# The first batch's last two slots as seven-product slots, and down_w's rounding behind them

## The chip, the cores and the metric

The kernel runs on one core of a Trainium2 chip. The metric is the device time of one execution in microseconds (us), lower is better; the time given for the kernel before is the median of three runs. One further execution was recorded by the hardware profiler, and all rows of the profile come from it.

The core has five engines with queues of their own: TensorE (PE: matmuls; its weight loads, PEld, overlap them), VectorE (DVE), ScalarE (ACT), GpSimd (POOL) and SyncE (SP, which here issues nearly all DMAs). Each runs its instructions in the order in which the kernel wrote them; semaphores order the engines against each other.

## The reference

```python
x (4,1024,512) f32, cond (4,128), norm_w (512,128), up_w (4096,512), down_w (512,2048)
scale = cond @ norm_w.T + 1.0
ms = mean(x * x, axis=-1)
h = x * (scale[:, None, :] * rsqrt(ms + 1e-6))
u = h @ up_w.T                       # 4096 columns: val, gate
val, gate = split(u, 2, axis=-1)
h = val * gelu(gate)                 # exact gelu, 2048 columns
s = 127 / max(|h|, axis=-1);  hq = clip(round(h * s), -128, 127) / s
m = mean(|down_w|);  wq = clip(round(down_w / m), -1, 1) * m
y = hq @ wq.T + x
```

So there is an up projection in full precision, a gated activation, and a down projection of whole numbers between -128 and 127 by weights of -1, 0 and 1.

## The kernel before, in words

**Tiles and loops.** The four batches of 1024 tokens are worked on one after the other, each in two halves of 512 tokens (`TOK`). The 2048 hidden columns are cut into 16 *slots* (`NJ`), slot j being 128 value rows and the 128 gate rows that belong to them. An fp32 product is made from f16 parts: each operand is split into a high and a low part, and high x low, low x high and high x high are added up, over a contraction of 512 in four pieces of 128. That is 12 matmuls (128x128 weights, 512 tokens) for one product of a slot: gate or value, first or second half, 48 matmuls a slot. This plain form is `plain` (matmuls L601), called by `plain_half` (product `pg` of the gate, Gelu on ScalarE L629, product `pv` of the value, then VectorE's value x gate, L633).

**The seven-product form.** From batch 1 on a slot is `slot`: the four products are seen as a 2x2 block product (two blocks of the contraction, two halves of tokens by value and gate) and formed from seven products of half the contraction, of 6 matmuls each (`product`, L586), 42 matmuls a slot. They need seven combinations of the weights and seven of the tokens. Three of each are the blocks themselves, four are sums or differences. The products 2 and 3 of a slot are done in the slot behind it. PSUM banks go by tag: A has two, B one, E two; the plain form uses the same ones (`pg` of the first half in B, of the second in A, `pv` in E; slot 6 has one of its own).

**Batch 0 is plain, and prepares the rest.** While its slots run, the other engines make what the later batches need. `first_batch(j)` is the order written out by hand for slot j; each of its steps works a few slots ahead:
- `w_range(j+3)`: the largest |weight| of each up_w row (VectorE reduce, L290), a power of two near it, and its inverse (L155, L297, L303); `w_gain` L317. `w_scale` (ScalarE, L329) scales the rows by it.
- `w_rows`: high part (ScalarE, L353) and low part (VectorE, L354) of the scaled rows, into a row tile (`ROW_SLOT`, a slot of the big buffer H), and a DMA transpose on SP (L355) into the slot's weight tile.
- `s_sums` (GpSimd, L380 to L383), `s_high` (ScalarE, L392), `s_low` (GpSimd, L396): the four weight sums with their high and low parts, and `s_spill` (SP, L400), which writes the whole set to `s_dram`; from there `s_load_x` and `s_load_y` fetch it for each later slot, two slots ahead.
- batch 1's tokens (`Tokens`, four pieces, at slots 6, 8, 10, 12 and the one after each): load, norm (Square on ScalarE, L520), scale, sums, high and low parts, and a transpose into batch 1's token tile.
- down_w: its eight pieces are loaded early, |down_w| is summed (`d_sum`, ScalarE, L448, two passes for two pieces), the mean is formed at slot 4 (`d_mean`, matmul L457), and in slots 5 to 12 each piece is rounded (`d_round`, ScalarE, L464) and put as sign into fp8 (`d_put`, ScalarE, L473), with a transpose into `wd`, the tile of the down projection's weights (L475).
- `pair_max`: the running largest |h| of the batch's tokens, by pairs of slots (`LARGEST`, VectorE, L719 to L726).

**The later batches.** In each slot of a later batch the spare time of VectorE and ScalarE is filled with the quantisation of the batch before, the running largest and the next tokens; `Filler` holds these steps in order and gives each place x, y, z of a slot as many as a budget in us admits. The down projection of the batch before comes in slots 10 to 13 of the batch.

Of the kernel before, what the change touches and what calls it, by code (L numbers as in the profile page):

```python
# [9 lines left out]
F32 = mybir.dt.float32  # L10
# [41 lines left out]
def glu_quant_kernel(  # L52
# [30 lines left out]
    DVE.memset(neghalf, -0.5)  # L83
    emask = cpool.tile([P, 2], I32, name="emask")
    DVE.memset(emask, EXPONENT)
    undo_up = cpool.tile([P, 2], F32, name="undo_up")
    DVE.memset(undo_up, 1.0 / W_UP)
    unmagic = cpool.tile([P, 1], F32, name="unmagic")
    DVE.memset(unmagic, -MAGIC)
    one = cpool.tile([P, 1], F32, name="one")  # L90
# [45 lines left out]
        "p (c w f) -> p c w f", c=7, w=2  # L136
    )
    A21 = R[:, 0, 6144 : 6144 + 768].bitcast(F16).rearrange("p (n w f) -> p n w f", n=3, w=2)

    def s_tile(g):  # L140


        if g >= NJ:
            return SXY[:, (g + 1) % 2]
        return S_more if g % 3 == 2 else SXY[:, g % 3]
# [129 lines left out]
    def wn(j):  # L275
        return H[:, W_EARLY.get(j, W_SLOT[j % 3])]
# [3 lines left out]
    def w_load(j, ts=(1, 0)):  # L280
# [3 lines left out]
        for t in ts:  # L284
            SP.dma_start(out=wn(j)[:, t], in_=up_v[j][:, t])

    def w_largest(j, t0=0, t1=2):
        t = slice(t0, t1)
        am = sm.tile([P, 2], F32, name=f"wam_{j}_{t0}", tag="wam")[:, t]
        DVE.tensor_reduce(am, wn(j)[:, t], AX.X, ALU.max, apply_absolute_value=True)  # L290
        return am

    def w_factor_steps(j, am, t0=0, t1=2):
        t = slice(t0, t1)
        pow2_floor(am)
        yield
        DVE.scalar_tensor_tensor(  # L297
            sw[:, j, t], am, 2.0**-100, undo_up[:, t], ALU.max, ALU.mult
        )
# [3 lines left out]
        DVE.reciprocal(iv[j][:, t], sw[:, j, t])  # L303
# [41 lines left out]

    def w_rows(j):

        v = H[:, ROW_SLOT.get(j, 15 + j % 2)].bitcast(F16).rearrange("p t d -> p (t d)")  # L350
        n = v.rearrange("p (n w f) -> p n w f", n=4, w=2)
        f = wn(j).rearrange("p t (n f) -> p (t n) f", n=2)
        ACT.copy(n[:, :, 0], f)  # L353
        DVE.tensor_tensor(n[:, :, 1], f, n[:, :, 0], ALU.subtract)  # L354
        SP.dma_start_transpose(  # L355
            s_tile(j)[:, 3:7].rearrange("p n w (k f) -> p (n w k) f", k=2), v
        )

    def w_high(j, ts=(1, 0)):
# [17 lines left out]
    def s_sums(j):  # L377
        v = wn(j).rearrange("p t (n f) -> p t n f", n=2)
        a11, a12, a21, a22 = v[:, 1, 0], v[:, 1, 1], v[:, 0, 0], v[:, 0, 1]
        POOL.tensor_tensor(sf[:, 0], a21, a22, ALU.add)  # L380
        POOL.tensor_tensor(sf[:, 2], a11, a21, ALU.subtract)
        POOL.tensor_tensor(sf[:, 1], sf[:, 0], a11, ALU.subtract)
        POOL.tensor_tensor(sf[:, 3], a12, sf[:, 1], ALU.subtract)  # L383
# [14 lines left out]
    def s_spill(j):  # L398
        def out(c0, c1, v):
            SP.dma_start(  # L400
                out=s_dram[j, :, c0 * 2 * HALF : c1 * 2 * HALF],
                in_=v.rearrange("p c w f -> p (c w f)"),
            )

        s = s_tile(j)
        if j < ROWS:
            out(0, C_ALL, s)
            return
        out(0, 3, s[:, 0:3])
        out(4, C_ALL, s[:, 4:])  # L410
        out(3, 4, A21[:, j % 3 : j % 3 + 1])

    def s_load(g, c0, c1, turn=False):
        s, d = s_tile(g)[:, c0:c1], s_dram[g % NJ, :, c0 * 2 * HALF : c1 * 2 * HALF]
# [2 lines left out]
        else:  # L417
            SP.dma_start(out=s.rearrange("p c w f -> p (c w f)"), in_=d)

    def s_load_x(g):  # L420
        s_load(g, Y_TO, C_ALL)
        s_load(g, 0, Y_FROM, True)

    def s_load_y(g):
# [10 lines left out]
    def d_part(n):  # L435
        return R[:, 1, n * HF : (n + 1) * HF]
# [18 lines left out]
    def d_mean(part):  # L455
# [2 lines left out]
        DVE.tensor_scalar(wmean, pm, 1.0 / (D * FF), 1e-5, ALU.mult, ALU.max)  # L458
        DVE.reciprocal(wsc, wmean)

    def d_round(n):

        dn = d_part(n)
        ACT.activation(dn, dn, AF.Copy, scale=wsc, bias=MAGIC)  # L464

    tn = []

    def d_put(n):
        _, u, y = d_at(n)
        if y == 0:  # L470
            tn.append(wpool.tile([P, HF], BF16, name=f"tn_{n}", tag="v"))
        t8 = tn[-1].bitcast(F8).rearrange("p (f y) -> p f y", y=2)
        ACT.activation(t8[:, :, y], d_part(n), AF.Sign, bias=unmagic, saturate=False)  # L473
        if y:
            SP.dma_start_transpose(wd[:, n // 4, u], tn[-1])  # L475

    def w_block(name):
        k, y = W_AT[name]
# [98 lines left out]

    TERMS = [(w, 1 - w, k) for w in (1, 0) for k in range(2)] + [(0, 0, k) for k in range(2)]

    def product(c, g, ps, start, stop):  # L580
        s = s_tile(g)[:, PLACE[c]]
        s = s.rearrange("p w (k f) -> p w k f", k=2)
        tv = t_view(g // NJ)
        o = ps.rearrange("p (a t) -> p a t", t=P)
        for n, (w, l, k) in enumerate(TERMS):
            PE.matmul(  # L586
                o, s[:, w, k, :], tv[:, :, c, l, k, :],
                start=start and n == 0, stop=stop and n == len(TERMS) - 1,
                skip_group_check=True,
            )  # L590

    def plain(j, t, h, ps):

        gate, a21, a22 = a_parts(j)
        a = [gate[:, 0], gate[:, 1]] if t else [a21, a22]
        a = [v.rearrange("p w (k f) -> p w k f", k=2) for v in a]
        terms = [(w, 1 - w, k) for k in range(NK) for w in (1, 0)]
        high = [(0, 0, k) for k in range(NK)]
        terms = high + terms if j < 2 else terms + high
        for n, (w, l, k) in enumerate(terms):  # L600
            PE.matmul(  # L601
                ps, a[k // 2][:, w, k % 2, :], XP[:, l, k, h * TOK : (h + 1) * TOK],
                start=n == 0, stop=n == len(terms) - 1,
            )

    sg = {0: sg0}

# [449 lines left out]
    def second_part():  # L1057
# [18 lines left out]
    LARGEST = {  # L1076
        4: ((0, 0), (0, 1)), 5: ((1, 0), (1, 1)), 8: ((2, 0), (2, 1)), 10: ((3, 0), (3, 1)),
        12: ((4, 0), (4, 1)), 14: ((5, 0), (5, 1)), 15: ((6, 0), (6, 1)),
    }
    toks = {}  # L1080

    def next_tokens(j):

# [9 lines left out]
    def first_batch(j, sc):  # L1093

        if j + 2 <= LATE:
            w_load(j + 4)
        if j >= 4:
            next_tokens(j + 2)
        t = toks.get(j)
        odd = t is not None and j not in TOKENS  # L1100
        n = j + 2
        rows = LATE <= n < NJ
        if j + 1 < LATE:
            s_sums(j + 1)
        elif rows:
            s_sums(n)
# [6 lines left out]
        for i, h in LARGEST.get(j, ()):  # L1113
            for f in pair_max(0, i, h):
                f()
        if n < LATE:
            w_scale(n)
            w_rows(n)
        if j + 1 < LATE:
            s_all(j + 1)  # L1120
        if t and not odd:
            t.norm()
        for m in D_ROUND.get(j, ()):
            d_round(m)
            d_put(m)
        if t and not odd:
            t.scale(sc)
            t.sums()
# [5 lines left out]
        if odd:  # L1134
            t.turn()
        plain_half(j, 1)
        if j == 3:
# [5 lines left out]
        own = rows and j + 1 >= LATE  # L1143

        def next_rows():
            if LATE <= j + 3 < NJ:
# [5 lines left out]
        if own:  # L1152
            s_high(n)
            s_low(n, POOL)
        if not odd:
            next_rows()
        if own:
# [4 lines left out]
            w_load(j + 5)  # L1162
        for n in D_SUM.get(j, ()):
            d_sum(n)
        if j in (NJ - 3, NJ - 1):
            s_load_x(NJ + (j - NJ + 3) // 2)
            s_load_y(NJ + (j - NJ + 3) // 2)


    def second_slot():  # L1170
# [62 lines left out]
    for n in D_SUM[2]:  # L1233
        d_sum(n)

    for j in range(3, NJ):
        if j == 5:
            sc = cond_load_scale(1)
        if j == 6:
            cond_bring(1, sc)  # L1240
        first_batch(j, sc if j >= 5 else None)

# [90 lines left out]
    state = {}  # L1333
    for b in range(1, B):
        dve, act = Filler(), Filler()
        gains(b)
        am = am_tile(b - 1)
        dq = state[b - 1] = sm.tile([P, 2 * NA], F32, name=f"dq_{b}", tag="dq")
        last_pair = NJ // 2 - 1
        for h in range(2):  # L1340
            add_pair(
# [38 lines left out]
        for j in range(NJ):  # L1380
# [11 lines left out]
            act_left = {"x": 2.7, "y": 2.2 if down else 1.1, "z": 0}  # L1392

            def run(p):
                nonlocal left
# [34 lines left out]

            def loads():
                if NJ + 2 <= g + 2 < B * NJ:
                    s_load_x(g + 2)
                if NJ + 2 <= g + 1 < B * NJ:
                    s_load_y(g + 1)


# [187 lines left out]
```

## Time and profile before

| what | value |
|---|---|
| median of 3 runs (lowest, highest) | 725.66 us (725.57, 725.80) |
| span of the profiled execution | 724.0 us |
| busy: PE, DVE, ACT, POOL | 716.5, 584.2, 397.6, 201.6 us |
| TensorE's share of the chain that ended last | 98% |
| a slot in plain form, on that chain | 4 x 2.59 = 10.36 us |
| slots 14 and 15 of batch 0 | 163.44 to 184.16 us |

The profile gives no total of its own beside the span, which runs from the first to the last recorded instruction; the runs' times hold what lies around it as well, 1.66 us by the median.

Rows of a timeline read: start, length, engine, line, operation, written tile <- read tiles, shape and type, and in brackets the idle time before it with what ended it. "x12" is a run of 12 such instructions in one row. Lines of tiles drop the buffer's number: H is the big buffer of activations and weights rows, SXY and R hold the slots' weight tiles. A row of the chain of waits reads: start, length, what. TensorE's granted clock is 1.00 in the stretches that are shown.

### The profile page before, as it was taken

To read this page: it belongs to the slowest core of one execution; us is meant where nothing else is said; L and a number is where in the kernel's file an instruction comes from. 1 tells how busy PE (TensorE), PEld (TensorE's weight loads), DVE (VectorE), ACT (ScalarE), POOL (GpSimd) and SP (SyncE) were. 2 spreads that over 40 slices of the span, in tenths; PEclk is the share of its full clock that TensorE was granted. 3 is DMA by queue.
4 is the path that set the end of the run, shared out by engine and by line. 5 is a ranking of instruction groups with operands and counts; after the bars stand their busy time and mean duration, and the time that the engine had idled before them with its cause. 6 is when DMAs were issued, how large, how long until landed. Compare 5 with 4: busy or idle time off the path is not lost.

```text
span 724.0 us, 10200 instructions
## 1 busy us (share of the span) xinstructions
PE 716.5 (99%) x3678; PEld 359.9 (50%) x3678; DVE 584.2 (81%) x824; ACT 397.6 (55%) x625; POOL 201.6 (28%) x207
## 2 busy tenths in 40 slices
PE   7999999999999999999999999999999999999998
PEld 3544444444444446655444445666444444445854
DVE  8977999984698899887689897687678888755896
ACT  6768868861337674554335676544433665333473
POOL 1579788882100034440000030360020000000120
PEclk9999999999999999999999999999999999999999
DMA  9579999996654564977846646766955455453253
GB/s 317 190 231 271 300 287 251 276 229 152 117 103 102 132 150 127 208 174 167 174 102 103 131 102 176 200 155 159 216 105 103 101 104 100 102 101 97 103 174 119
DMA packets 224191, 117.85 MB, mean 163 GB/s; under 512 B 186486, under 2 KB 196871, under 8 KB 224140
## 3 DMA queue, kind: packets, MB, share of 16 engines
q1 hardware_dynamic: 223850, 116.87, 66.1%
q8 instruction: 29, 0.48, 0.3%
q10 hardware_dynamic: 290, 0.33, 0.1%
q14 instruction: 22, 0.18, 0.1%
HBM read 49.50 MB, written 23.09 MB: 100 GB/s over the span
## 4 chain that ended last, share of the span: by engine, by line
PE 98%; DMA 1%; ACT 0%; SPq 0%; issue 0%; DVE 0%; ACTq 0%
PE A L586 34%; PE E L586 17%; PE pg L601 11%; PE pv L601 11%; PE po L880 9%; PE B L586 9%; PE po_end L832 4%; DMA H<-in_x_dram 1%; PE ptx L981 1%; PE pv L648 0%; PE po_B L880 0%; PE pg L648 0%; PE pw L339 0%; PE po_A L880 0%; PE po_E L880 0%; ACT R L947 0%
## 5 line engine op out<-in xcount | busy, mean ns | idle before, releaser
L586 PEld LDWEIGHTS <-SXY 128*128 128x128 f16 x2016 | 196.9, 98 | 231.3 <-issue 0.6
L586 PE MATMUL A<-R,SXY 128*128 128x512 f16 x1152 | 266.0, 379 | 0.0
L586 PE MATMUL E<-R,SXY 128*128 128x512 f16 x576 | 140.0, 379 | 0.1
L688 DVE SCALAR_TENSOR_TENSOR H<-A,sg,t 128x512 f32<-128x512 f32 x48 | 36.0, 750 | 67.9 <-PE A L586 67.7
L740 POOL PARTITION_ALL_REDUCE am<-R x8 | 14.3, 1793 | 234.0 <-DVE R L726 234.0
L804 DVE TENSOR_TENSOR H<-H,am 128x1024 f32<-128x1024 f32 x64 | 76.1, 1215 | 0.0
L601 PEld LDWEIGHTS <-SXY 128*128 128x128 f16 x486 | 47.4, 98 | 57.4 <-DVE SXY L372 0.5
L701 ACT ACTIVATE t<-t,sg 128x512 f32<-128x512 f32 x48 | 34.6, 721 | 67.8 <-DVE t L698 67.7
L586 PE MATMUL B<-R,SXY 128*128 128x512 f16 x288 | 70.0, 379 | 0.0
L724 DVE TENSOR_REDUCE gm<-H 128x512 f32<-128x1024 f32 x56 | 69.0, 1233 | 1.0
L601 PE MATMUL pg<-R,SXY 128*128 128x512 f16 x252 | 58.0, 379 | 0.0
L601 PE MATMUL pv<-R,SXY 128*128 128x512 f16 x234 | 54.4, 380 | 0.0
L685 ACT ACTIVATE t<-B,sg 128x512 f32<-128x512 f32 x48 | 33.0, 687 | 36.3 <-PE B L586 36.3
L880 PE MATMUL po<-wd,R 128*128 128x256 fp8e4 x416 | 52.5, 273 | 0.0
L490 POOL TENSOR_SCALAR ssq<-ssq 128x2 f32<-128x2 f32 x12 | 4.3, 354 | 171.2 <-ACT xt L520 122.1
L668 ACT COPY t<-A 128x512 f32<-128x512 f32 x48 | 27.9, 582 | 39.8 <-PE A L586 39.5
L880 PEld LDWEIGHTS <-R 128*128 128x128 bf16 (+1 forms) x448 | 43.8, 98 | 9.0
L680 ACT COPY v<-E 128x512 f32<-128x512 f32 x48 | 28.1, 585 | 30.9 <-PE E L586 27.7
L675 ACT COPY B<-A 128x512 f32<-128x512 f32 x48 | 27.4, 572 | 30.5 <-PE A L586 30.0
L707 DVE SCALAR_TENSOR_TENSOR H<-v,sg,t 128x512 f32<-128x512 f32 x48 | 38.5, 802 | 6.6 <-ACT t L701 6.6
L812 ACT ACTIVATE H<-H 128x1024 f32<-128x1024 f32 x38 | 39.9, 1050 | 7.1 <-DVE H L804 7.1
L726 DVE TENSOR_TENSOR R<-R,gm 128x512 f32<-128x512 f32 x56 | 42.2, 753 | 1.3
(205 smaller groups left out, 986.8 us busy)
## 6 DMA issues: line engine op xcount, KB each, us to landing
SXY<-s_dram SPq DMA_DIRECT2D x48, 256.0 KB, 3.0
s_dram<-SXY SPq DMA_DIRECT2D x18, 384.0 KB, 3.3
H<-in_L_cond_up_w_dram SPq DMA_DIRECT2D x13, 512.0 KB, 5.7
SXY<-s_dram SPq DMA_DIRECT2D x48, 128.0 KB, 3.2
xr<-in_x_dram SPq DMA_DIRECT2D x19, 256.0 KB, 3.0
out_dram<-xr SPq DMA_DIRECT2D x19, 256.0 KB, 2.6
H<-in_x_dram SPq DMA_DIRECT2D x8, 512.0 KB, 6.7
R<-in_L_cond_down_w_dram SPq DMA_DIRECT2D x8, 512.0 KB, 7.4
```

Of the source, the lines that this page charges most:

```text
L586: PE.matmul(o, s[:, w, k, :], tv[:, :, c, l, k, :], start=start and n == 0, stop=stop and n == len(TERMS) - 1, skip_group_check=True,)
L601: PE.matmul(ps, a[k // 2][:, w, k % 2, :], XP[:, l, k, h * TOK : (h + 1) * TOK], start=n == 0, stop=n == len(terms) - 1,)
L685: ACT.activation(cur["t1"], pb, AF.Gelu, scale=gain(g, 1))
L688: DVE.scalar_tensor_tensor(h_half(g - 1, 0), prev["A"], gain(g - 1, 0), prev["t1"], ALU.mult, ALU.mult)
L701: ACT.activation(prev["t2"], prev["t2"], AF.Gelu, scale=gain(g - 1, 1))
L707: DVE.scalar_tensor_tensor(h_half(g - 1, 1), prev["v"], gain(g - 1, 0), prev["t2"], ALU.mult, ALU.mult)
L724: DVE.tensor_reduce(gm[0], v, AX.X, ALU.max, apply_absolute_value=True)
L726: return [largest, lambda: DVE.tensor_tensor(m, m, gm[0], ALU.max)]
L804: DVE.tensor_tensor(v, v, r.to_broadcast([P, 2, TOK]), ALU.mult)
L812: ACT.activation(v, v, AF.Copy, bias=MAGIC)
L832: PE.matmul(po.rearrange("p (y c o) -> p y c o", c=2, o=P), q[:, a, h, j], wd8[:, :, j // n, j % n, :, y0:y1].rearrange("p c o y -> p y c o"),
L880: PE.matmul(po, w[:, j], m, start=start and j == 0, stop=stop and j == n - 1, skip_group_check=True,)
```

## The change

Slots 14 and 15 of batch 0 (`FAST = NJ - 2`) go through `slot` instead of `plain_half`. What moves for it:
- Token sums of batch 0: four combinations, high and low, in `T0`, which is the memory of `wd`; they are formed at slots 4 to 14 (`T0_STEPS` and `first_fast`) by VectorE, GpSimd and ScalarE. The three plain combinations are read where they stand (`XP`).
- Weight sums of slots 14 and 15 are formed on VectorE instead of GpSimd, and turned by DMA transposes from SBUF (`s_turn`), beside the spill. `w_rows` of these two turns three of its four parts.
- `wd` is thus not free before slot 15. down_w is fetched again, piece by piece, and rounded and signed from slot 14 to slot 19 (`first_fast`, and `D_LATE` in ScalarE's Filler), with the transposes at slots 16, 17, 18 and 20, between the loads (`D_MOVES`).
- From weights 3 on (`BY_SUM`) the range is taken from the sum of |w| of a row instead of its largest: two Abs with accumulation on ScalarE in place of VectorE's reduce. Their elementwise output goes to the row tile of `row_place(j)`. The gain of two slots is formed in one instruction.
- Batch 1's tokens come one slot earlier (5, 7, 9, 11), some of the running largest a slot earlier or later.

```diff
+    FAST = NJ - 2
+    T0 = wd.bitcast(F16).rearrange("p a b c d -> p (a b c d)")
...
+    BY_SUM = 3
+
+    def row_place(j):
+        return H[:, ROW_SLOT.get(j, 15 + j % 2)]
+
     def w_largest(j, t0=0, t1=2):
         t = slice(t0, t1)
         am = sm.tile([P, 2], F32, name=f"wam_{j}_{t0}", tag="wam")[:, t]
+        if j >= BY_SUM:
+            for n in range(2):
+                jk = row_place(j).bitcast(F16)[:, n, :D]
+                ACT.activation(jk, wn(j)[:, n], AF.Abs, accum_out=am[:, n : n + 1])
+            return am
         DVE.tensor_reduce(am, wn(j)[:, t], AX.X, ALU.max, apply_absolute_value=True)
         return am
...
     def w_gain(j):
-        DVE.tensor_tensor(sg0[:, j, :], sw[:, j, :], dx[:, 0:1].to_broadcast([P, 2]), ALU.mult)
+        if j < 3:
+            DVE.tensor_tensor(sg0[:, j, :], sw[:, j, :], dx[:, 0:1].to_broadcast([P, 2]), ALU.mult)
+        elif j % 2 == 0 or j == NJ - 1:
+            c = slice(j - 1, j + 1)
+            DVE.tensor_scalar(sg0[:, c], sw[:, c], dx[:, 0:1], None, ALU.mult)
...
+    def s_turn(j):
+        for n in range(2):
+            SP.dma_start_transpose(
+                s_tile(j)[:, 2 * n : 2 * n + 2].rearrange("p c w (k f) -> p (c w k) f", k=2),
+                s_rows[j][n].rearrange("p c w f -> p (c w f)"),
+            )
...
+    FIRST = {0: (0, 0), 1: (2, 0), 2: (2, 1)}
+
+    def operand(b, c, l, k):
+        if b:
+            return t_view(b)[:, :, c, l, k, :]
+        if c in FIRST:
+            k0, h = FIRST[c]
+            v = XP[:, l, k0 + k, h * TOK : (h + 1) * TOK]
+        else:
+            v = T0[:, c - 3, l, k]
+        return v.rearrange("p (a t) -> p a t", t=P)
...
-    D_ROUND = {5: (0, 1), 6: (2,), 7: (3,), 9: (4,), 10: (5,), 11: (6,), 12: (7,)}
+    D_LATE = [
+        ((0, "x"), d_round, 2), ((0, "x"), d_sign, 2), ((0, "y"), d_round, 3),
+        ((1, "x"), d_sign, 3), ((1, "x"), d_round, 4), ((1, "y"), d_sign, 4),
+        ((2, "x"), d_round, 5), ((2, "x"), d_sign, 5), ((2, "y"), d_round, 6),
+        ((3, "x"), d_sign, 6), ((3, "x"), d_round, 7), ((3, "y"), d_sign, 7),
+    ]
+    D_MOVES = {
+        0: ((d_turn, 0),),
+        1: ((d_turn, 1), (d_fetch, 6)),
+        2: ((d_turn, 2), (d_fetch, 7)),
+        4: ((d_turn, 3),),
+    }
+    T0_STEPS = {
+        (4, 0): [lambda: t0_whole(0, 0, 0), lambda: t0_whole(1, 0, 1)],
+        (4, 1): [lambda: t0_sum(2, 1, 0, ALU.subtract)],
+        (5, 0): [lambda: t0_high(2, 1)],
+        (6, 0): [lambda: t0_low(2, 1)],
+        (6, 1): [lambda: t0_whole(2, 2, 1, POOL)],
+        (8, 0): [lambda: t0_sum(1, 2, 1, ALU.subtract)],
+        (8, 1): [lambda: t0_high(1, 3)],
+        (9, 1): [lambda: t0_low(1, 3)],
+        (10, 0): [lambda: t0_sum(0, 1, 0, ALU.add)],
+        (10, 1): [lambda: t0_high(0, 2)],
+        (11, 0): [lambda: t0_low(0, 2)],
+        (12, 1): [lambda: t0_whole(3, 2, 0, POOL)],
+        (13, 0): [lambda: t0_sum(3, 3, 0, ALU.subtract)],
+    }
     D_MEAN = 4
-    TOKENS = {6: 0, 8: 1, 10: 2, 12: 3}
+    TOKENS = {5: 0, 7: 1, 9: 2, 11: 3}
...
+    def first_fast(j):
+
+        last = j == NJ - 1
+
+        def x():
+            if last:
+                d_round(1)
+                d_sign(0)
+            else:
+                d_round(0)
+
+        def y():
+            if last:
+                d_sign(1)
+            else:
+                t0_high(3, 0)
+
+        def z():
+            if not last:
+                t0_low(3, 0)
+            largest(j)
+
+        slot(j, x, y, z)
+        if last:
+            s_load_x(j + 2)
+            d_fetch(4)
+            d_fetch(5)
+        else:
+            d_fetch(2)
+            d_fetch(3)
...
-    for j in range(3, NJ):
+    for j in range(3, FAST):
...
+    for j in range(FAST, NJ):
+        first_fast(j)
```

`t0_whole` and `t0_sum` are one add or subtract of 128x1024 f32 each, `t0_high` a copy to f16 on ScalarE, `t0_low` the difference between the sum and its high part on VectorE. `D_MOVES` steps run inside `s_load_x` between its two loads; `d_sign` writes what `d_put` wrote, and `d_turn` is its transpose.

More of the change, by code (lines that the diff above doesn't have):

```diff
@@ L459, in d_mean, with d_fetch, d_sign, d_turn @@
         DVE.reciprocal(wsc, wmean)
[L461 to L475 removed]
+    dn = {}
+    tn = {}
+    def d_fetch(n):
+        if n == 2:
+            v = H[:, NJ].rearrange("p h t -> p (h t)")
+        else:
+            tag = ("xn", "xt", None, "nx", "xn", "xt", "nx", "xn")[n]
+            v = wpool.tile([P, HF], F32, name=f"dn_{n}", tag=tag, bufs=1)
+        c, u, _ = d_at(n)
+        SP.dma_start(out=v, in_=down_w[c * P : (c + 1) * P, u * HF : (u + 1) * HF])
+        dn[n] = v
+    def d_round(n):
+        ACT.activation(dn[n], dn[n], AF.Copy, scale=wsc, bias=MAGIC)
+    def d_sign(n):
+        y = n % 2
+        if y == 0:
+            tn[n // 2] = wpool.tile([P, HF], BF16, name=f"tn_{n}", tag="xr")
+        t8 = tn[n // 2].bitcast(F8).rearrange("p (f y) -> p f y", y=2)
+        ACT.activation(t8[:, :, y], dn[n], AF.Sign, bias=unmagic, saturate=False)
+    def d_turn(m):
+        SP.dma_start_transpose(wd[:, m // 2, m % 2], tn[m])
     def w_block(name):
@@ L604, in plain, with t0_whole, t0_sum, t0_high @@
             )
+    TMP = [R[:, 1, n : n + 2 * TOK].rearrange("p (k t) -> p k t", k=2) for n in (7168, 5376, 3584)]
+    TMP.append(H[:, 15])
+    def t0_whole(m, k0, h, eng=DVE):
+        v = XP[:, :, k0 : k0 + 2, h * TOK : (h + 1) * TOK]
+        eng.tensor_tensor(TMP[m], v[:, 0], v[:, 1], ALU.add)
+    def t0_sum(o, m, l, op, eng=DVE):
+        eng.tensor_tensor(TMP[o], TMP[m], TMP[l], op)
+    def t0_high(o, c):
+        ACT.copy(T0[:, c, 0], TMP[o])
+    def t0_low(o, c, eng=DVE):
+        eng.tensor_tensor(T0[:, c, 1], TMP[o], T0[:, c, 0], ALU.subtract)
     sg = {0: sg0}
@@ L1105, in first_batch @@
         elif rows:
-            s_sums(n)
+            s_sums(n, DVE if n >= FAST else POOL)
         if j + 3 < NJ:
@@ L1120, in first_batch @@
             s_all(j + 1)
+        if j + 2 == FAST:
+            s_high(FAST)
+            s_low(FAST, POOL)
+            s_turn(FAST)
+        if j == 12:
+            d_fetch(0)
         if t and not odd:
             t.norm()
-        for m in D_ROUND.get(j, ()):
-            d_round(m)
-            d_put(m)
         if t and not odd:
             t.scale(sc)
-            t.sums()
+            if j < 11:
+                t.sums()
         if j + 2 > LATE and j + 5 < NJ:
@@ L1133, in first_batch @@
             t.low(DVE)
-        if odd:
+        if odd and j + 2 < FAST:
             t.turn()
         plain_half(j, 1)
+        for f in T0_STEPS.get((j, 1), ()):
+            f()
+        if j + 2 == FAST:
+            s_spill(FAST)
+        if j + 2 > FAST:
+            s_high(j + 2)
+            s_low(j + 2, POOL)
+            s_turn(j + 2)
+            d_fetch(1)
+            s_spill(j + 2)
+            toks[j - 1].turn()
         if j == 3:
@@ L1142, in first_batch @@
             d_mean(part)
-        own = rows and j + 1 >= LATE
+        own = rows and j + 1 >= LATE and not ahead
+        rows = rows and not ahead
         def next_rows():
@@ L1335, in glu_quant_kernel @@
         dve, act = Filler(), Filler()
-        gains(b)
+        if b > 1:
+            gains(b)
         am = am_tile(b - 1)
         dq = state[b - 1] = sm.tile([P, 2 * NA], F32, name=f"dq_{b}", tag="dq")
+        if b == 1:
+            for at, f, n in D_LATE:
+                act.add(at, 1.1, lambda now, f=f, n=n: f(n))
         last_pair = NJ // 2 - 1
```

90 lines of the change are left out of this document (60 added, 30 removed).

## The prediction

> **What bounds the kernel now.** I read the page's head and chain first, then the chain of waits around the two slots, then the same chain and the engines' timelines where the preparation of the first batch is densest. The page (engine rows: busy time, share of the span, instructions):
>
> ```profile
> span 724.0 us, 10200 instructions
> ...
> PE 716.5 (99%) x3678; PEld 359.9 (50%) x3678; DVE 584.2 (81%) x824; ACT 397.6 (55%) x625; POOL 201.6 (28%) x207
> ...
> PE 98%; DMA 1%; ACT 0%; SPq 0%; issue 0%; DVE 0%; ACTq 0%
> ```
>
> TensorE carries 98% of the chain that ends last: a matmul taken away is time won, and any new wait of TensorE is time lost. The chain at the two slots that change (start, length, what; us):
>
> ```profile
> 163.44 2.59 PE pg L601 x12
> 166.03 2.59 PE pv L601 x12
> ...
> 181.57 2.59 PE pv L601 x12
> 184.16 1.29 PE A L586 x6
> ```
>
> Slots 14 and 15 run from 163.44 to 184.16 without a gap, eight products of 12 matmuls, 2.59 us each.
>
> **The saving.** The two slots go from 2 x 48 matmuls (four products of 12) to 2 x 42 (seven of 6), and the operands keep their shape, so one matmul keeps its price: 2.59 / 12 = 0.216 us plain, 1.29 / 6 = 0.215 us in the scheme. 12 x 0.216 = 2.59 us. If TensorE waits nowhere, 725.66 - 2.59 = 723.07 us. The profiled execution spans 724.0, so 1.66 us lie around the span of the median run; I take them as unchanged.
>
> What it costs must therefore be a wait of TensorE. The engines' busy time by stretch (window, then PE, PEld, DVE, ACT, POOL, granted clock, DMA share, GB/s):
>
> ```profile
> 60.00:70.00 10.00, 10.00 (x49) 4.67 (x48) 7.63 (x13) 9.90 (x18) 8.61 (x9) 1.00 0.99 304
> 70.00:80.00 10.00, 10.00 (x50) 4.57 (x49) 9.86 (x14) 8.69 (x12) 9.15 (x12) 1.00 1.09 290
> 170.00:180.00 10.00, 10.00 (x48) 4.56 (x47) 4.94 (x7) 1.37 (x2) 0.38 (x1) 1.00 0.50 108
> ```
>
> At 60 to 70 us ScalarE has 0.1 us of 10 to spare, at 170 to 180 it has 8.6. The change adds ScalarE work in the first place and moves other ScalarE work to the second.
>
> **Weight ranges on ScalarE.** From slot 3's weights on, one reduce of VectorE becomes two Abs with accumulation on ScalarE. The nearest rows are the Square pair of the token norms, the same 128x512 with accumulation, and the reduce it replaces:
>
> ```profile
> 83.77 0.62 ACT L520 ACTIVATE xt<-xn 128x512 f32<-128x512 f32 x1
> ...
> 85.00 1.14 ACT L464 ACTIVATE R<-R,wsc 128x1024 f32<-128x1024 f32 x1
> ```
>
> ```profile
> 47.60 1.21 DVE L290 TENSOR_REDUCE wam<-H 128x2 f32<-128x1024 f32 x1
> ...
> 52.90 1.20 DVE L354 TENSOR_TENSOR H<-H 128x1024 f16<-128x1024 f32 x1
> ```
>
> The Square pair at 83.77 occupies 1.23 us until the next one at 85.00; I take 1.23 for each range. 13 x 1.23 = 16.0 us go onto ScalarE, 13 x 1.21 = 15.7 us leave VectorE. Through slots 5 to 12 this is nearly paid by the 16 rounding passes that leave ScalarE there (1.14 each, the row at 85.00). In slots 2 to 4 nothing leaves. So I follow ScalarE's queue there:
>
> ```profile
> 42.77 1.33 ACT L329 ACTIVATE H<-H,iv 128x512 f32<-128x512 f32 x2 [3.41 <-DVE iv L303]
> ...
> 46.23 0.67 ACT L629 ACTIVATE g<-pg,sg 128x512 f32<-128x512 f32 x1
> 46.80 1.03 ACT L353 CAST H<-H 128x1024 f16<-128x1024 f32 x1
> 47.74 1.14 ACT L392 CAST R<-H 128x768 f16<-128x768 f32 x2
> 48.78 1.05 ACT L448 ACTIVATE djk<-R 128x1024 bf16<-128x1024 f32 x1
> ...
> 51.01 0.67 ACT L629 ACTIVATE g<-pg,sg 128x512 f32<-128x512 f32 x1
> 52.99 0.83 ACT L392 CAST SXY<-H 128x768 f16<-128x768 f32 x1 [1.31 <-POOL H L382]
> 54.73 0.41 ACT L392 CAST R<-H 128x256 f16<-128x256 f32 x1 [0.91 <-POOL H L383]
> ```
>
> The ranges of weights 3 and 4 fall where ScalarE stood idle (3.41 us before 42.77), and cost nothing; by my count ScalarE even reaches the scaling of weights 4 some 0.2 us early. The range of weights 5 comes behind the gate's gelu: 46.0 + 0.57 + 1.23 = 47.8. Then, by the rows' spacings: high part 0.95, sums' high part of slot 2 1.04, two |down_w| passes 2.23 (51.01 - 48.78), so the next gelu at 52.0 instead of 51.01. The sums' high part of slot 3 waits for GpSimd, whose last two sums these are:
>
> ```profile
> 52.23 0.72 POOL L382 TENSOR_TENSOR H<-H 128x256 f32<-128x256 f32 x1
> 53.03 1.66 POOL L383 TENSOR_TENSOR H<-H 128x256 f32<-128x256 f32 x1
> ```
>
> GpSimd's third sum ended at 52.95. It follows the low part of slot 2, which waits for the high part that now comes 1.0 later: 54.0. The row at 53.03 took 1.66 instead of 0.72 while VectorE's two-input row ran (52.90, 1.20). In the new kernel VectorE loses the reduce at 47.60 and gets to that subtraction about 1.0 us earlier, at 51.9 to 53.1, amid the first three sums of GpSimd. So I count one such delay, 1.2 us, ahead of the third sum: 55.2. Then high part 0.73 + 0.31, the same two passes 2.23, range of weights 6 1.23: slot 3's first gelu at 59.7, done 60.4.
>
> The Trainium skill, page "SBUF — State Buffer", section "Who interferes with whom", says that VectorE and GpSimd share a port pair as an exclusive lock held for a whole instruction; that a VectorE instruction with two SBUF inputs contends with GpSimd's reads; and that a tensor_reduce on trn2 never does. That speaks against this change: it takes out 13 reduces and puts in 18 two-input instructions (10 on tokens, 8 on weight sums). The trace agrees in the pair 1.66 against 0.72. By the rule the delay of 1.2 us is due and the sum is the one below; by the free duration alone it would be 723.4 (rival 1).
>
> Who waits for that gelu is the next gate product, which takes the same single bank (B). TensorE's rows:
>
> ```profile
> 59.54 2.75 PE L601 MATMUL pg<-R,SXY 128*128 128x512 f16 x12
> ...
> 70.04 2.75 PE L601 MATMUL pg<-R 128*128 128x512 f16 x12
> ```
>
> Slot 4 starts at 60.4 instead of 59.54: 0.9 us.
>
> **A new wait of ScalarE.** The Abs results are thrown away into the row tile of an earlier weight block; for weights 7 that is the tile that the transpose of weights 5 reads (H[16]). So the range of weights 7 waits until this transpose has landed. Queued behind it on ScalarE is slot 4's first gelu, and bank B passes the wait to slot 5's first product. Issue rows of SP, landings (last column, us):
>
> ```profile
> 61.90 3.63 SPq L355 DMA_TRANSPOSE R<-H  x1
> ...
> 71.54 0.48 SPq L512 DMA_DIRECT2D xn<-in_x_dram  x1
> ```
>
> ```profile
> R<-H SPq DMA_TRANSPOSE x9, 6.5
> SXY<-H SPq DMA_TRANSPOSE x9, 4.3
> ```
>
> After slot 3's gelu starts at 59.7: 0.57, scaling 1.33, high part with its full 1.03, to 62.6; VectorE's low part 1.20 and 0.4, my allowance for what SP is issuing just then: 64.2. The landing is bounded by 4.3 and 6.5; no row shows this one alone, so I take the middle, 5.4: 69.6. ScalarE's own queue (0.57, 1.33, 0.95, sums 1.04, gelu 0.57, scaling 1.33, high 0.95, two passes 2.23) is there at 68.7, so the transpose ends last. Range 1.23, gelu 0.67: 71.5. Slot 5 starts at 71.5 instead of 70.04, which holds the first 0.9: **1.5 us in all** (0.6 with a landing of 4.3, when ScalarE's own queue decides; 2.6 with 6.5).
>
> **The rest, costed at nothing, with its cover.**
> - VectorE in slots 4 to 8: two whole sums and two more token steps come in, about 1.2 each (52.90), and the next tokens one slot earlier; three reduces of 1.21 leave. About +2 us in a stretch 99% busy (70 to 80). Evacuations have a spare bank and now 1.5 us of delay to hide in. Uncovered it would cost up to 0.5.
> - Token and weight sums of slots 10 to 15: VectorE has half of 170 to 180 free. The last weight rows should land some 1 us ahead of their use at 171.2, the last token sum about 0.8 ahead of 173.8, both unshifted. Without cover: up to 1 us.
> - Rounding in slots 14 to 19: 16 passes of 1.14 = 18.2 us into a stretch where ScalarE is busy 1.37 of 10. A pass started just ahead of a copy that TensorE needs could hold it by 1.14; I expect 0 to 0.5, taken as 0.
> - SP: eight down_w fetches (0.5 to 0.9 us of issue) and the transposes move to slots 12 to 20, where the DMA share is 0.50. The first token load moves ahead of the transpose of weights 5 (it stood at 71.54, behind it), and takes part of its DMA time: this is in the upper landing.
> - The pairing of gains takes about seven small VectorE rows out; no gain counted.
>
> Sum: 725.66 - 2.59 + 1.5 = 724.57, taken as **724.6 us** (span about 722.9).
>
> **Rivals.**
> 1. *The lag is absorbed.* GpSimd's third sum isn't delayed, or the transpose lands in under 5.1 us. Without the delay everything after 54.0 comes 1.2 earlier: transpose issued 63.0, landed 68.4, gelu done 70.3, wait 0.3: 723.4 us. For it: before, the delay hit the fourth sum only, and the 9.90 of ScalarE includes passes nobody waits for. Against it: the counting puts VectorE's subtraction amid the sums. Chance 0.37.
> 2. *The transpose of weights 5 lands late.* Same place, other side. The token load (512 KB) now goes ahead of it with the DMA share at 0.99. With L the time to landing, the wait is 64.2 + L + 1.9 - 70.04; it uses up the saving at L = 6.5 and costs 0.2% from L = 8.0 (wait over 4.0). As far above 6.5 as 4.3 lies below it, L is 8.7; at 8.4 the wait is 4.5, 727.6 us. For it: the 6.5 median. Against it: the 4.3 of the other nine. With smaller waits in VectorE's stretch added, chance 0.20.
> 3. *VectorE becomes the bound in slots 4 to 8.* +2 us with the delay not covering it: 723.07 + 2 = 725.1. For it: 9.86 of 10. Against it: the reduces leave early, just before. Chance 0.06, within 0.2%.
>
> **How the numbers follow.** The forecast has 0.37, rivals 1 to 3 0.37, 0.20 and 0.06. 0.2% is 1.45 us, about what a measurement tells from no change: faster is below 724.2, slower above 727.1. Faster 0.37 (rival 1), same 0.43 (forecast and rival 3), slower 0.20. The forecast's own range is 724.2 to 725.7 (landing 5.1 to 6.5). For 8 in 10 the range reaches to 723.0 (no wait) and to 727.6 (rival 2 at its price); above that little is left.
>
> **What would show it.** TensorE's matmul rows fall by 12, and the chain from slot 14 to 16 is 18.1 us instead of 20.7. In the chain of waits, slot 4's first product starts about 0.9 later behind a gelu, slot 5's 1.5 later, with a ScalarE wait on the transpose's DMA before the range of weights 7. GpSimd's sums of slot 3 show one row near 1.7 to 1.9. Slots 14 to 19 show no TensorE gap over 0.5 us. I'm wrong if the gap lies elsewhere, most likely in slots 6 to 8 behind VectorE, or at 171 to 180 behind the new rows' transposes.

## The result, and the profile after

The changed kernel takes 736.3 us (median of 4 runs, 735.27 to 737.17), the kernel before took 725.73 beside it: a ratio of 1.0145, 95% interval 1.0131 to 1.0159. It is 10.6 us slower where 1.1 us faster was forecast. The profiled execution spans 735.4 us against 724.0. Of the four runs of the changed kernel two, the profiled one among them, show a mean granted clock of 0.997 and took 737.0 and 737.2 us, and two show 1.000 and took 735.3 and 735.6, which suggests that the slow groups of matmuls at slot 16, below, are not in every execution.

The page of the changed kernel (span, busy time, the chain that ended last by engine):

```profile
span 735.4 us, 10237 instructions
...
PE 718.5 (98%) x3666; PEld 359.4 (49%) x3666; DVE 590.7 (80%) x828; ACT 419.4 (57%) x687; POOL 204.8 (28%) x201
...
PE 80%; POOL 6%; DVE 6%; DMA 2%; SPq 2%; issue 2%; ACT 1%; POOLq 0%; DVEq 0%; ACTq 0%
```

The 12 matmuls are gone (3678 to 3666 rows), but the chain is no longer TensorE's alone: 12% of it runs through GpSimd and VectorE. TensorE's timeline shows where (start, length, and in brackets the wait before it and what ended it):

```profile
59.91 2.75 PE L667 MATMUL pg<-R,SXY 128*128 128x512 f16 x12
...
70.49 2.75 PE L667 MATMUL pg<-R 128*128 128x512 f16 x12
...
100.56 2.75 PE L667 MATMUL pv<-R,SXY 128*128 128x512 f16 x12 [1.41 <-DVE H L715]
104.51 2.75 PE L667 MATMUL pg<-R 128*128 128x512 f16 x12 [1.21 <-ACT g L711]
...
173.16 1.46 PE L652 MATMUL A<-R 128*128 128x512 f16 x6
...
187.56 1.46 PE L652 MATMUL A<-wd,SXY 128*128 128x512 f16 x6
191.03 2.23 PE L652 MATMUL A<-R,SXY 128*128 128x512 f16 x6 [2.01 <-DMA SXY<-s_dram]
193.46 2.20 PE L652 MATMUL E<-R,SXY 128*128 128x512 f16 x6 [0.20 <-DMA SXY<-s_dram]
```

Slots 4 and 5, where the forecast put 1.5 us of waiting, start at 59.91 and 70.49: 0.4 later than before, 0.35 of which were there before the ranges of slots 4 and 5 matter (the same product started at 38.19 before and 38.54 after). The waits begin in slot 7 and come back nearly every slot, behind VectorE's value x gate (L715) or a gelu (L711, ScalarE). Slot 14 starts at 173.16 instead of 163.28: **9.9 us**. Then 12 matmuls less give 2.6 back, and slot 16 waits 2.2 us for its weights, after which two groups of six matmuls take 2.23 and 2.20 us instead of 1.46: **4.2 us** with the small gaps. 9.9 - 2.6 + 4.2 = 11.5; the spans differ by 11.4.

What VectorE and GpSimd do ahead of the first waits, their timelines side by side, VectorE first:

```profile
93.54 2.69 DVE L686 TENSOR_TENSOR wd<-R,wd 128x1024 f16<-128x1024 f32 x1
96.15 2.02 DVE L624 TENSOR_TENSOR nx<-xn,nx 128x512 f16<-128x512 f32 x2
98.10 1.74 DVE L624 TENSOR_TENSOR nx<-xt,nx 128x1024 f16<-128x1024 f32 x1
99.76 0.74 DVE L715 SCALAR_TENSOR_TENSOR H<-pv,sg,g 128x512 f32<-128x512 f32 x1
100.42 1.21 DVE L375 TENSOR_TENSOR H<-H 128x1024 f16<-128x1024 f32 x1
```

```profile
93.51 1.64 POOL L426 TENSOR_TENSOR SXY<-H,SXY 128x768 f16<-128x768 f32 x1
95.11 1.65 POOL L426 TENSOR_TENSOR R<-H,R 128x256 f16<-128x256 f32 x1
96.72 1.17 POOL L402 TENSOR_TENSOR H<-H 128x256 f32<-128x256 f32 x1
97.86 0.90 POOL L403 TENSOR_TENSOR H<-H 128x256 f32<-128x256 f32 x1
98.72 1.70 POOL L404 TENSOR_TENSOR H<-H 128x256 f32<-128x256 f32 x1
100.50 1.71 POOL L405 TENSOR_TENSOR H<-H 128x256 f32<-128x256 f32 x1
```

L686 is the low part of a token sum, one of the ten VectorE instructions that the change adds. It starts 0.03 us behind the start of a GpSimd instruction of 1.64 and takes 2.69 instead of 1.21; then GpSimd's next one takes 1.65 where 0.67 is its length when undisturbed, and so on. The two engines work in turn. At the end of this sequence VectorE's value x gate (99.76) is late, and TensorE waits for it (100.56); GpSimd's last sum ends at 102.21, ScalarE's high part waits for it, the gelu stands behind that, and TensorE waits again (104.51).

### The profile page after: what moved, and what is told of

It is laid out like the page before. It is cut to its first block, busy times and chain, and to the rows that moved or that the text cites. A ratio compares the mean times of both kernels' runs of the same rounds, so it can differ in the third digit from the quotient of the medians.

```text
span 735.4 us, 10237 instructions
## 1 busy us (share of the span) xinstructions
PE 718.5 (98%) x3666; PEld 359.4 (49%) x3666; DVE 590.7 (80%) x828; ACT 419.4 (57%) x687; POOL 204.8 (28%) x201
## 4 chain that ended last, share of the span: by engine, by line
PE 80%; POOL 6%; DVE 6%; DMA 2%; SPq 2%; issue 2%; ACT 1%; POOLq 0%; DVEq 0%; ACTq 0%
PE A L652 33%; PE E L652 17%; PE po L962 9%; PE B L652 8%; PE po_end L914 4%; PE pg L667 4%; PE pv L667 4%; DVE gm L806 1%; DMA H<-in_x_dram 1%; POOL R L426 1%; SPq L627 1%; POOL H L405 1%; POOL H L404 1%; DMA s_dram<-s_rows 1%; POOL xt L597 1%
## 5 line engine op out<-in xcount | busy, mean ns | idle before, releaser
L652 PE MATMUL E<-R,SXY 128*128 128x512 f16 x582 | 142.2, 380 | 0.3 <-DMA SXY<-s_dram 0.2
L770 DVE SCALAR_TENSOR_TENSOR H<-A,sg,t 128x512 f32<-128x512 f32 x50 | 37.5, 750 | 70.8 <-PE A L652 70.6
L783 ACT ACTIVATE t<-t,sg 128x512 f32<-128x512 f32 x50 | 36.1, 721 | 67.6 <-DVE t L780 67.5
L652 PE MATMUL B<-R,SXY 128*128 128x512 f16 x294 | 71.5, 379 | 0.0
L667 PE MATMUL pg<-R,SXY 128*128 128x512 f16 x228 | 52.4, 379 | 2.3 <-ACT g L711 2.3
L667 PE MATMUL pv<-R,SXY 128*128 128x512 f16 x210 | 48.9, 379 | 3.0 <-DVE H L715 3.0
```

Of the source, the lines that this page charges most:

```text
L652: PE.matmul(o, s[:, w, k, :], operand(g // NJ, c, l, k), start=start and n == 0, stop=stop and n == len(TERMS) - 1, skip_group_check=True,)
L667: PE.matmul(ps, a[k // 2][:, w, k % 2, :], XP[:, l, k, h * TOK : (h + 1) * TOK], start=n == 0, stop=n == len(terms) - 1,)
L770: DVE.scalar_tensor_tensor(h_half(g - 1, 0), prev["A"], gain(g - 1, 0), prev["t1"], ALU.mult, ALU.mult)
L783: ACT.activation(prev["t2"], prev["t2"], AF.Gelu, scale=gain(g - 1, 1))
```

## The experiments

Two theories at first. **A (work):** in slots 7 to 13 VectorE and GpSimd have too much to do between them, because of the token sums. **B (queue):** the order on ScalarE is at fault: gelu behind Abs, Abs behind the weight sums' high part, that behind GpSimd, while VectorE idles for the Abs. VectorE did idle for it (16.7 us in 8 waits). Behind each time below stand, in brackets, its ratio to the kernel before, which ran beside it, and the 95% interval of that ratio.

**The ranges back on VectorE.**

```diff
-    BY_SUM = 3
+    BY_SUM = NJ
```

> The changed kernel with the weights' ranges taken from VectorE's reduce again, as before the change; all else as changed. Theory A (work: in slots 7 to 13 VectorE and GpSimd have too much to do between them, because of the token sums): VectorE gets 13 x 1.21 us more, so no faster than 736, up to 745. Theory B (queue: slots 7 to 13 wait because a gate's gelu stands on ScalarE behind the Abs, the Abs behind the weight sums' high part, and that behind GpSimd, while VectorE idles for the Abs): most of the 9.4 us of waits go, 727 to 732.

736.8 us (ratio 1.0155, 1.0140 to 1.0170). Taking the Abs off ScalarE wins nothing, which speaks against B as the whole cause. VectorE's idle time goes into the reduces, and TensorE then waits for VectorE's value x gate, slot after slot. Since the edit also gives VectorE its 15.7 us of reduces back, it doesn't exclude a share of B.

**No token sums.**

```diff
-    T0_STEPS = { ... }
+    T0_STEPS = {}
-    FIRST = {0: (0, 0), 1: (2, 0), 2: (2, 1)}
+    FIRST = {0: (0, 0), 1: (2, 0), 2: (2, 1), 3: (0, 1), 4: (0, 0), 5: (2, 0), 6: (2, 1)}
...
```

The two token-sum steps in `first_fast` are left out as well.

> The changed kernel with the token sums of batch 0 left out (12 adds, subtracts and low parts of 128x1024 on VectorE and GpSimd, 4 high parts on ScalarE); the products that use them read the plain token blocks instead, so the two slots' values are not the reference's. Theory A (work): the waits of slots 7 to 13 go, and what follows is on time: 723 to 727. Theory B (queue): the order on ScalarE is untouched, 731 to 736.

728.4 us (1.0036, 1.0023 to 1.0049), 7.9 us less than the changed kernel. Between slots 5 and 12 no wait of TensorE over 0.2 us is left; one of 1.0 in slot 13 and those around slot 16 stay. The order on ScalarE is as in the changed kernel, so the order by itself doesn't make the waits: for A, though 1.4 us above its range, because slot 16 is still late.

**The Abs ahead.** In `first_batch`, ahead of `s_high(n)`:

```diff
+        if own and j + 4 < NJ:
+            early_am[j + 4] = w_largest(j + 4)
         if own:
             s_high(n)
```

> The changed kernel with only the two Abs of weights 9 to 15 issued earlier on ScalarE, ahead of the weight sums' high part instead of behind it. Theory A (work): as much work for VectorE and GpSimd as in the changed kernel, 735 to 737. Theory B (queue): the gelu and VectorE's range no longer wait for GpSimd through the Abs, 729 to 733.

741.7 us (1.0217, 1.0201 to 1.0232): slower than either said. The waits of ScalarE in slots 6 to 14 name a third thing:

```profile
ACT H L308 <- DMA SXY<-H: 13.2, 2, 7.5
...
ACT H L308 <- DMA R<-H: 6.0, 2, 4.5
```

The early Abs wait 19 us for transposes that still read the row tile into which they throw their output. This is the wait that the prediction put at slot 5; in the changed kernel it comes at 135.3 and 158.7 us, 2.3 and 1.9 long, and is nearly hidden. The run couldn't decide on B.

**No late rounding.** `d_fetch`, `d_round`, `d_sign` and `d_turn` do nothing, except for one memset:

```diff
     def d_turn(m):
-        SP.dma_start_transpose(wd[:, m // 2, m % 2], tn[m])
+        if m == 3:
+            POOL.memset(wd, 0.0)
```

> The changed kernel with the second fetch of down_w, its rounding, signs and transposes left out (slots 12 to 20); one GpSimd memset of the weight tile stands in their place, so the output is x alone. It shows what the moved rounding costs. Both theories put the waits of slots 7 to 13 elsewhere (9.4 us, stay). If the 4 us at the start of slot 16 come from the moved fetches and rounding: 732 to 733; if they are only the lateness of the last weight rows and tokens handed on: 735 to 737.

740.2 us (1.0196, 1.0179 to 1.0213): neither. Slot 16 had no wait any more, but the stand-in memset cost more than what it stood for (last section): TensorE waits 5.32 us for VectorE behind it. So the run was repeated below with the memset in four parts.

**One input instead of two.** With A ahead, the question is what the token sums cost: VectorE's time (D), or that VectorE and GpSimd work in turn (C). Each of the ten VectorE instructions of the token sums becomes a reduce:

```diff
-        eng.tensor_tensor(T0[:, c, 1], TMP[o], T0[:, c, 0], ALU.subtract)
+        DVE.tensor_reduce(jk, XP[:, 0, 0:2, :TOK], AX.X, ALU.max, apply_absolute_value=True)
```

> The changed kernel with each of VectorE's ten token-sum instructions replaced by a reduce of 128x1024, which has one input and about the same length (1.2 us); the two GpSimd adds and the four ScalarE copies stay; the products read plain token blocks, so the two slots' values are not the reference's. Theory C (in turn: a VectorE instruction with two inputs and a GpSimd instruction never run at once, so the token sums cost both engines their length): as without the sums, 728 to 731. Theory D (full: VectorE simply has no time for ten more instructions, whatever they are): as the changed kernel, 734 to 737.

729.4 us (1.0058, 1.0041 to 1.0075). Ten instructions of the same undisturbed length, and 6.9 of the 7.9 us are gone (by the medians). The group of the replacements, and busy time from 70 to 160 us, this run's and then the changed kernel's (PE, PEld, DVE, ACT, POOL, clock, DMA share, GB/s):

```profile
L679 DVE TENSOR_REDUCE one<-R x10: 1201/1209/1222, 72.2 to 172.8; 128x2 f32<-128x1024 f16 x10
...
70.00:160.00 90.00, 88.66 (x409) 39.80 (x408) 83.64 (x101) 66.05 (x126) 77.28 (x78) 1.00 0.95 242
```

```profile
70.00:160.00 90.00, 82.95 (x381) 36.98 (x379) 80.63 (x93) 61.31 (x119) 78.89 (x73) 1.00 0.85 225
```

VectorE is busier here (83.64 of 90) than in the changed kernel (80.63), in which a good part of the busy time was waiting inside instructions. This is what C expects, and against D.

**No late rounding, with the memset in four.**

```diff
-        if m == 3:
-            POOL.memset(wd, 0.0)
+        POOL.memset(wd[:, m // 2, m % 2], 0.0)
```

> As the run without the late rounding, but with the single GpSimd memset of 7.00 us, which held VectorE for 6.59 us and TensorE for 5.49, cut into four smaller ones at the places of the four transposes. If the 4 us at the start of slot 16 come from the moved fetches and rounding: 732 to 733.5. If that run's early start of slot 16 was chance: 736.

734.9 us (1.0130, 1.0114 to 1.0145). Slot 16 starts without a wait. The four small memsets run one right behind the other, 3.69 us in all, and hold VectorE again; TensorE waits for it at 209.5 us and loses 2.2 us with the gaps. Taken off, 732.7: by this subtraction the late fetch and rounding cost some 3.6 us, most of the 4.2 at slot 16.

**The Abs output apart.**

```diff
-                jk = row_place(j).bitcast(F16)[:, n, :D]
+                jk = wpool.tile([P, TOK], F32, name=f"jk_{j}_{n}", tag="t2").bitcast(F16)[:, :D]
```

> The changed kernel with the thrown-away output of the Abs written to a tile that nobody reads instead of the row tile, so that no Abs waits for a transpose to land. If that wait costs time in the changed kernel (the prediction's step): 732 to 735. If it is hidden: 735.5 to 737.

735.9 us (1.0145, 1.0130 to 1.0161): hidden. The waits of slots 7 to 13 are the same to 0.03 us.

**The Abs ahead, with their output apart.** Both edits together.

> The Abs issued ahead of the weight sums' high part, as before, but their output written to the tile that nobody reads. Theory B (queue), which the first try could not test because the early Abs waited 19 us in all for transposes: 729 to 733. Theory A (work for VectorE and GpSimd): 735 to 738.

737.9 us (1.0178, 1.0159 to 1.0198): no faster than the changed kernel. The Abs no longer wait for transposes, but the edit brings a new wait: they now come before the load of their weights has landed (7.6 us in 3 waits of ScalarE, the longest 5.2). In slot 7 TensorE loses some 8.7 us, 6.44 of waiting and a group of twelve slower by 2.15:

```profile
95.76 2.75 PE L671 MATMUL pg<-R,SXY 128*128 128x512 f16 x12
104.95 4.90 PE L671 MATMUL pv<-R,SXY 128*128 128x512 f16 x12 [6.44 <-DVE H L719]
109.69 2.75 PE L671 MATMUL pg<-R 128*128 128x512 f16 x12
```

From there to the third product of slot 12 no wait is left, where the changed kernel has 4.6 us of them; but the other engines had the 8.7 us to get ahead. So this run doesn't decide on B either. That the order on ScalarE is not the whole cause is shown by the run without the token sums; whether it makes them dearer is open.

**Neither sums nor late rounding.** The edits of the second and the sixth experiment together.

> The changed kernel with both left out: batch 0's token sums (plain blocks read instead) and the late fetch and rounding of down_w (four small GpSimd memsets instead), so the output is not the reference's. If these two hold all that the change costs, the 12 matmuls less show: 723 to 724.5. If the ranges on ScalarE, the earlier tokens or the weight rows of the two slots cost something by themselves: 725 to 728.

727.0 us (1.0022, 1.0007 to 1.0036), 2.5 above the first range. The profile shows why:

```profile
195.84 2.75 PE L655 MATMUL A<-R,SXY 128*128 128x512 f16 x12
200.61 2.30 PE L655 MATMUL E<-R,SXY 128*128 128x512 f16 x6 [2.02 <-DVE t L783]
202.70 2.35 PE L655 MATMUL B<-R,SXY 128*128 128x512 f16 x6
204.88 1.46 PE L655 MATMUL A<-R,SXY 128*128 128x512 f16 x6
```

That is the stand-in memset again: 2.2 us of waiting and two groups slower by 0.8 and 0.9, 3.9 in all. Taken off the 727.4 of this execution, 723.5; the time before, 725.5 beside it, less 12 matmuls is 722.9. The sum is worked out, not run; by it the two things left out hold all of the loss but some 0.6 us.

**Ten instructions more in the kernel before.** To see the cost of the token sums by itself, ten unused instructions go into the old kernel at the places of the ten, with two inputs or with one:

```diff
+        DVE.tensor_tensor(o.bitcast(F16), R[:, 0, 0:1024], R[:, 0, 1024:2048], ALU.add)
```

```diff
+        DVE.tensor_reduce(o, R[:, 0, 0:1024].rearrange("p (k t) -> p k t", k=2), AX.X, ALU.max, apply_absolute_value=True)
```

> The kernel before, with ten unused VectorE adds put at the places in slots 4 to 14 where the change puts its token sums: 128x1024 f32, two inputs, f16 out. Theory C (in turn with GpSimd): 728 to 735. Theory D (VectorE full): the same as the next run.

> The kernel before, with ten unused VectorE reduces of 128x1024 f32 (one input, 1.2 us) at the same places. Theory C (in turn with GpSimd): 725.5 to 727. Theory D (VectorE full): 728 to 735, as the run with two inputs.

730.1 us with two inputs (1.0069, 1.0050 to 1.0087), 726.2 with one (1.0013, 1.0002 to 1.0024).

**One of the two inputs from PSUM.** Reduces and adds differ in more than their inputs. So the adds again, with their large output, but one input in a PSUM bank that ScalarE fills once a slot:

```diff
+            ACT.copy(ps, R[:, 0, 0:TOK])
...
+        a = mores.pop().rearrange("p (o t) -> p o t", o=1).to_broadcast([P, 2, TOK])
+        DVE.tensor_tensor(o, a, b, ALU.add)
```

> The kernel before, with ten unused VectorE adds of 128x1024 in slots 4 to 14 as in the run with two inputs, but one of the two inputs lies in PSUM (a bank that ScalarE fills once a slot, 0.6 us; the one of slot 6 moved to slot 7). If it is the second input from SBUF that makes VectorE and GpSimd take turns: as with the one-input reduces, 725.5 to 727.5. If it is the adds as such (their kind, their written output): as with two inputs from SBUF, 729 to 732.

726.1 us (1.0008, 0.9999 to 1.0017). The ten instructions' durations in ns (shortest/median/longest), two inputs from SBUF, then one of them from PSUM:

```profile
L1099 DVE TENSOR_TENSOR more<-R x10: 1214/1664/2683, 71.8 to 181.7; 128x1024 f16<-128x1024 f32 x10
```

```profile
L1108 DVE TENSOR_TENSOR more_o<-more,R x10: 1207/1208/1219, 70.6 to 176.3; 128x1024 f16<-128x1024 f32 x10
```

The same add, the same output: with both inputs in SBUF it takes up to 2683 ns and the kernel 4.6 us longer than before (725.5 beside it); with one in PSUM it takes 1207 to 1219 every time, and the interval of the kernel's ratio takes in 1. It is the second input from SBUF. These ten cost the kernel before less (4.6 us) than the sums cost the changed kernel (7.9); what makes the difference was not run.

**The fetch behind the spill.** What makes slot 16 late? In the changed kernel the high part of slot 15's sums waits for the spill of slot 14's to land, whose tile it takes, and that spill stands behind the first late fetch on SP (SP's timeline, then ScalarE's):

```profile
168.30 0.57 SPq L516 DMA_DIRECT2D dn<-in_L_cond_down_w_dram  x1
168.92 0.90 SPq L430 DMA_DIRECT2D s_dram<-s_rows  x2
```

```profile
174.09 1.27 ACT L422 CAST s_rows<-H 128x512 f16<-128x512 f32 x2 [2.64 <-DMA s_dram<-s_rows]
```

```diff
-        if j == 12:
-            d_fetch(0)
...
         if j + 2 == FAST:
             s_spill(FAST)
+            d_fetch(0)
```

> The changed kernel with the first late fetch of down_w (512 KB) issued behind the spill of slot 14's weight sums instead of ahead of it. ScalarE's high part of slot 15's sums waited 2.64 us for that spill to land. If the fetch ahead of it is what makes slot 16 late: the 4 us there shrink to under 2, 733 to 735. If not: 735.5 to 737.

734.4 us (1.0122, 1.0107 to 1.0137), 1.9 less than the changed kernel. Its TensorE at slots 16 and 17:

```profile
188.25 1.47 PE L652 MATMUL A<-R,SXY 128*128 128x512 f16 x6 [0.49 <-DMA SXY<-s_dram]
...
197.31 2.75 PE L652 MATMUL A<-R,SXY 128*128 128x512 f16 x12 [0.85 <-ACT t L750]
```

The wait shrinks from 2.01 to 0.49 and the matmuls behind it run at full speed. A new wait of 0.85 comes six products later, behind a ScalarE copy that stands in the queue behind two rounding passes of 1.15 us: there the late rounding shows itself.

No run here beats the kernel before. Token sums with one input in PSUM and the fetch moved would be the version to try; if the one-input run's 6.9 us and the 1.9 here add up, which is an estimate, it comes to 727.5, still above 725.7; it was not built.

## Why the prediction was wrong, step by step

- **The saving** was right: 12 rows less, and by the run with neither cost the time comes within some 0.6 us of it (worked out, above). The sign "18.1 us from slot 14 to 16" was miscounted: two of slot 15's seven products are done in slot 16, so twelve groups of six lie between the two starts, 15.5 us without waits; with them it was 17.9.
- **ScalarE's queue in slots 2 to 4** was right to some tenths, as long as ScalarE alone is counted: the second gelu of slot 2 was forecast for 52.0, slot 3's first for 59.7. ScalarE's timeline of the changed kernel:

```profile
52.02 0.67 ACT L711 ACTIVATE g<-pg,sg 128x512 f32<-128x512 f32 x1
54.62 0.83 ACT L422 CAST SXY<-H 128x768 f16<-128x768 f32 x1 [1.94 <-POOL H L404]
...
59.20 0.67 ACT L711 ACTIVATE g<-pg,sg 128x512 f32<-128x512 f32 x1
```

  GpSimd's third sum was ready at 54.6 instead of 55.2: VectorE's subtraction ran at 49.20, earlier than I counted, and met GpSimd's low part (2.89 instead of 2.27 us), so the delay was 0.6 and not 1.2. Slot 3's gelu ended at 59.87 instead of 60.4, and slot 4's first product, itself 0.35 late from earlier, had nothing to wait for.
- **The wait for the transpose of weights 5** did not come: it was issued at 63.49 (forecast 64.2), and the range of weights 7 ran at 68.23, right behind the |down_w| passes, without an idle row. So the tile was free within 4.7 us; the 4.3 and 6.5 of the prediction were medians of nine transfers each and no bounds. Here rival 1 was right, "the lag is absorbed". The mechanism itself exists, as the Abs issued early showed; in the changed kernel it costs about 0.4 us at most (736.3 against 735.9).
- **The failing step** is the first bullet of what was costed at nothing: VectorE in slots 4 to 8, "About +2 us in a stretch 99% busy", of which "up to 0.5" would be uncovered. It priced the token sums by VectorE's own time, 1.2 us each, for five slots. (Five reduces leave these slots, at 65.79 to 103.19 in the profile before, and not three, so VectorE's own time hardly grew.) With both inputs in SBUF each also stops GpSimd, or stands behind it. The second bullet has the same fault: it took VectorE's free time in slots 10 to 15 from 170 to 180 us, where GpSimd is busy 0.38 of 10, but four of the ten instructions run between 116 and 154, in slots 9 to 12. The kernel before, from 70 to 160 us and from 140 to 150 (busy time of PE, PEld, DVE, ACT, POOL):

```profile
70.00:160.00 90.00, 90.00 (x420) 40.79 (x419) 82.72 (x107) 69.75 (x104) 75.19 (x79) 1.00 1.05 265
...
140.00:150.00 10.00, 10.00 (x48) 4.57 (x47) 9.69 (x13) 8.15 (x13) 9.70 (x10) 1.00 1.12 266
```

  VectorE is busy 82.72 of 90 us and GpSimd 75.19. Two engines that must partly take turns had little such time left. The sums cost 7.9 us, 6.9 of them through the second input. Rival 3 had the engine right, but with 2 us, in slots 4 to 8, and at a chance of 0.06. The prediction's own sign of being wrong, a gap in slots 6 to 8 behind VectorE, is where the waits begin.
- The rule was in the prediction: the Trainium skill, page "SBUF — State Buffer", section "Who interferes with whom", and the eighteen new two-input instructions were counted. I then applied it to a single instruction in slot 3. Applied to all, it names the cause, though not the price: the ten added to the kernel before cost 4.6 us with two inputs from SBUF, 0.7 as reduces with one, and 0.6 with one of two in PSUM. The rule names inputs from SBUF only, and the trace agrees: with one of the two in PSUM the median is 1208 ns against 1664.
- **SP** was also costed at nothing. The prediction moved the fetches to a place where the DMA share was 0.50 and didn't ask what each goes ahead of. The first one stands ahead of a spill that the weight sums of slot 15 wait for: 1.9 us. All of the late fetch and rounding costs about 3.6.
- **Rounding against ScalarE's copies** (0 to 0.5, taken as 0): no such wait in the changed kernel, but 0.85 us as soon as slot 16 is on time.
- The range ended at 727.6 because each term was bounded alone. None of the rivals reached slots 9 to 13, where TensorE waits 5.6 of the 9.9 us.

## What to carry to other kernels

Where VectorE and GpSimd are both busy, an added VectorE instruction with two inputs from SBUF is to be charged to both engines; count GpSimd's busy share of the stretch before calling VectorE's spare time free. An operand in PSUM, or a reduce with its one input, took the charge away here: 1.2 us instead of 1.2 to 2.7 each. One input is no warrant by itself: see the tensor_scalar below. And when a transfer moves, read which later wait ends on the transfer right behind it in the queue.

## What was not expected of the hardware

- A GpSimd memset, which reads nothing, held a VectorE instruction with a single input for its whole length (VectorE's row, then GpSimd's, in the first run without late rounding; the instruction otherwise takes 0.36 to 0.39 us):

```profile
203.41 6.59 DVE L831 TENSOR_SCALAR am<-am 128x512 f32<-128x512 f32 x1
```

```profile
202.72 7.00 POOL L534 MEMSET wd<- 128x8192 bf16 x1
```

- After a wait of 2.0 us TensorE's next two groups of six took 2.23 and 2.20 us instead of 1.46 (at 191.03 in the changed kernel; the granted clock from 190 to 200 was 0.83). In the run with one input a wait of 2.29 us at the same place was followed by the usual 1.47. Behind the four small memsets a wait of 2.02 us was followed by 2.30 and 2.35 in the run with neither cost, and by the usual 1.46 in the run without the late rounding alone. What decides is open.
